# Turning the rows of three norms by DMA on 16-bit planes, in a transformer stack on one Trainium2 core

## The chip, the cores and the metric

One Trainium2 chip, one of its cores. A core has TensorE (PE: matrix products, with results in PSUM), VectorE (DVE), ScalarE (ACT), GpSimd (POOL) and SyncE (SP), which issues DMAs; each engine works through its own queue in order, and they wait for each other through semaphores. The metric is the time of one execution in microseconds (us), as the median of several runs.

## The reference

The input is `x` of 8 sequences x 1024 rows x 256 values, float32. Four layers follow each other, each as a residual over a norm without gain:

```python
x = x + _L0_attn_ref(_layernorm(x), ...)   # linear ("flow") attention + its own FFN of 1024
x = x + _L0_ffn_ref(_layernorm(x), ...)    # relu FFN of 1024
x = x + _L1_attn_ref(_layernorm(x), ...)   # softmax attention over 1024 rows
x = x + _L1_ffn_ref(_layernorm(x), ...)    # gated FFN of 704, operands rounded to blocks of FP4
```

The first layer is a whole decoder layer: attention with cumulative sums along the rows, `h = layernorm(inputs + attn)`, `ffn = gelu(h @ W1 + b1) @ W2 + b2`, and `layernorm(h + ffn)`. All of it is computed in float32 here; only the FP4 rounding uses 16-bit helpers.

## The kernel before

The rows are worked on in chunks of 128 (one row a partition) and in groups of four chunks: 8 sequences x 2 groups = 16 flows. A matmul needs its contraction along the partitions, so a block of rows `[128, 256]` that has just been normed has to be turned into two blocks `[128 features, 128 rows]` before the next layer can multiply it. `turned` does this with two TensorE transpositions against an identity into a PSUM bank, and ScalarE copies the bank into an SBUF tile.

Three such places are touched by the change:

- `linear_chunk`, the first norm after attention: `h` is turned into tile `half` (kind `hT`), the operand of the GELU FFN;
- `norms_1`, the second: `n` is turned into `half` (kind `nT`), the operand of the relu FFN. Both go through `turn_half`;
- `norms_2`, the third: `n` is turned into `n2T`, the operand of the softmax attention, first of all of the values' matmul with `wv3`.

Three other turns stay on TensorE in both kernels: `n0T` ahead of the linear attention, the rows of the FP4 layer, and the probabilities.

`dense` runs both FFNs. For each half group (two chunks, 256 rows) it takes eight steps: a first matmul (`bank<-half,w_in`), an activation into `hidden`, and two steps later a second matmul (`bank<-w_out,hidden`) into an accumulator that is kept over the eight. The weights don't stay in SBUF: each step loads a `w_in` and a `w_out` tile of 128 KB, `W_FF` = 5 tiles of each kind ahead. The linear attention has `V_PADS` = 5 tiles of values, so at most five chunks are between their values and their attention.

Nothing here is scheduled by the hardware or by a compiler. The kernel is written as some hundred Python generators ("parts"), each of which yields what it needs next: an engine, the tiles that must be ready, and how many PSUM banks. `Plan.run` keeps a clock for each engine, made from the costs in `Plan.took`, and picks the part that can go on soonest. `RIPE` says how long an operand should have been ready by that clock, and `at` gives a due time. What is picked is emitted at once, and the order of each engine is pinned to the order of emission. So a cost in `took` doesn't change an instruction; it changes the order. Where the clock sees TensorE pausing for more than 1.6 us, `fill` emits products of the identity with itself that keep the engine running.

Every DMA is issued from SyncE's queue, in order, with eight completion semaphores taken in turn: a DMA also waits for the one that used its semaphore before. In the profile nearly all instructions carry the line of the recording helper (L337), so they are told apart by their tiles.

Of the kernel before, what the change touches and what calls it, by code (L numbers as in the profile page):

```python
# [9 lines left out]
F32 = mybir.dt.float32  # L10
I32 = mybir.dt.int32
BF16 = mybir.dt.bfloat16
AF = mybir.ActivationFunctionType
ALU = mybir.AluOpType
AX = mybir.AxisListType
# [5 lines left out]
FF = 1024  # L21
NF = FF // P
INTER = 704
V_PADS = 5
W_FF = 5
RES = 10
HALVES = 5
LAG = 2
# [24 lines left out]
    "rows": (4, D, F32),  # L53
    "hid": (3, INTER_PAD, F32),
    "q_c": (2, INTER, BF16),
}


# [4 lines left out]
class Plan:  # L63
# [96 lines left out]
    def took(self, queue, op, args, kw):  # L160

        aps = [x for x in list(args) + list(kw.values()) if isinstance(x, bass.AP)]
        outs = [kw["out"] if "out" in kw else aps[0]]
        if kw.get("accum_out") is not None:
            outs.append(kw["accum_out"])
        size = 1
        for ap in aps:
            n = 1
            for d in ap.shape[1:]:
                n *= d  # L170
            size = max(size, n)

        overlap, after = 0.0, 0.035
        if queue == "tensor":
            size = 1
            for d in outs[0].shape[1:]:
                size *= d
            cost = size * (0.853e-3 if op == "transpose" else 1.687e-3)
            tiled = op == "matmul" and (kw["lhsT"].shape[-1] <= 32 or kw["lhsT"].shape[0] <= 32)
            if tiled or op == "matmul" and kw["lhsT"].dtype == BF16:  # L180
                cost *= 0.25
            if tiled != self.tiled:
                cost += 0.2
            self.tiled = tiled
            after = 0.2
        elif queue == "vector":
            each = {"reciprocal": 6.2e-3, "tensor_tensor_scan": 2.15e-3}.get(op, 1.05e-3)
            cost = 0.17 + each * size
            if op == "tensor_scalar" and outs[0].dtype == BF16:
                cost = 0.16 + 0.26e-3 * size  # L190
            elif op == "scalar_tensor_tensor" and any(ap.shape[-1] == 1 for ap in aps):
                cost += 0.06
            overlap = 0.08
        elif queue == "scalar":
            cost = (0.16 if op == "copy" else 0.26) + 0.82e-3 * size
            for x in args:
                if not isinstance(x, bass.AP) and self.SETS.get(x, self.act_set) != self.act_set:
                    self.act_set = self.SETS[x]
                    self.free[queue] = self.free.get(queue, 0.0) + 1.3
            if kw.get("accum_out") is not None:  # L200
                cost += 0.15
            overlap = 0.1
        elif queue == "gpsimd":
            cost = 0.65 + 0.7e-3 * size
            if op in ("tensor_scalar", "iota"):
                cost = 0.22
            elif op == "memset":
                cost = 0.1 + 0.9e-3 * size
        else:
            cost = 0.4  # L210
        start = self.free.get(queue, 0.0)
        if queue not in ("tensor", "sync"):
            start = max([start] + [self.used.get(ap.tensor.name, 0.0) for ap in outs])
        for ap in aps:
            name = ap.tensor.name
            if self.by.get(name) != queue or queue in ("vector", "gpsimd"):
                start = max(start, self.done.get(name, 0.0) + (0.05 if queue == "gpsimd" else 0.0))
            if name not in self.done and name in self.held:
                start = max(start, self.used[name])
        if queue == "tensor":  # L220
            if start - self.ran > 2.0:
                self.slow = start + 2.1
            if start < self.slow:
                cost *= 2
            self.ran = start + cost
        if queue == "sync":
            start = max(start, self.landed.pop(0))
        end = start + cost
        if queue == "sync":
            n = 4e-6 / 250e-3  # L230
            for d in outs[0].shape:
                n *= d
            self.free["rings"] = max(self.free.get("rings", 0.0), end) + n
            after = self.free["rings"] - end + 2.1
            self.landed.append(end + after)
        self.free[queue] = end - overlap
        for ap in outs:
            self.done[ap.tensor.name] = end + after
            self.by[ap.tensor.name] = queue
        for ap in aps:  # L240
            name = ap.tensor.name
            self.used[name] = max(self.used.get(name, 0.0), end + after)
            if queue != "tensor" and name not in self.kept:
                self.held.discard(name)
# [17 lines left out]
    def act(self, *tiles, **kw):  # L262
        return self.need("scalar", tiles, **kw)
# [92 lines left out]
def block_stack_kernel(ctx: ExitStack, tc: tile.TileContext, a: dict, out: bass.AP):  # L356
# [268 lines left out]
    def turned(srcs):  # L625

        bank = tr_bank()
        for i, src in enumerate(srcs):
            nc.tensor.transpose(bank[:, i, :], src, ident)
        return bank[:, : len(srcs), :]  # L630

    def table(func):


        if plan.act_set != plan.SETS.get(func, plan.act_set):
            nc.scalar.activation(small([P, 1], "table", 1), one, func)

    def halves(t):
        return [t[:, 0:P], t[:, P : 2 * P]]
# [259 lines left out]
    def turn_half(p, kind, i, src):  # L899
        dst = half_of(p, kind, i // 2)  # L900
        j = i % 2
        bank = turned(halves(src))
        plan.drop(src)
        yield act(bank)
        nc.scalar.copy(dst[:, :, j * P : (j + 1) * P], bank)
        n = groups[p]["turned"]
        n[kind, i // 2] = n.get((kind, i // 2), 0) + 1

# [218 lines left out]
    def linear_chunk(p, i, n0T, comp, qk):  # L1127
# [171 lines left out]
        for k in range(2):  # L1299
# [8 lines left out]
        plan.drop(u)  # L1308
        yield plan.pool(h)
        nc.gpsimd.tensor_tensor(rc, h, b2, ALU.add)  # L1310
        yield pe(
            h,
            banks=1,
            at=at + 0.74 + 0.06 * i,
            when=lambda: half_fits(p, "hT", i // 2) and count["dense"] >= p - 1,
        )
# [124 lines left out]
    def norms_1(p, i, acc, taken):  # L1441

        s, c = divmod(p * G + i, NCH)
        xc = groups[p]["res"][i]
        xr = yield from fresh("xr", dma())
        nc.sync.dma_start(out=xr, in_=x_dram[s, c * P : (c + 1) * P, :])
        u = yield from fresh("norm", dve(acc, when=lambda: "norms" in late), "u")
        nc.vector.tensor_tensor(u, acc, xc, ALU.add)
        taken()
        stats = ln_stats(u)  # L1450
        yield plan.pool(xr)
        nc.gpsimd.tensor_tensor(xr, xr, ln2b, ALU.add)
        yield from layernorm_affine(xc, u, ln2g, xr, stats)
        plan.drop(u, xr)
        yield dve(xc)
        n = yield from layernorm("norm", xc)
        yield plan.pool(xc, unused=(xc,))
        nc.gpsimd.tensor_tensor(xc, xc, fb2, ALU.add)
        yield pe(n, banks=1, when=lambda: half_fits(p, "nT", i // 2))
        yield from turn_half(p, "nT", i, n)  # L1460

    def norms_2(p, i, acc, taken):

        s, g = divmod(p, NG)
        q, xc = seqs[s], groups[p]["res"][i]
        yield dve(acc)
        nc.vector.tensor_tensor(xc, acc, xc, ALU.add)
        taken()
        yield dve(xc)
        n = yield from layernorm("norm", xc)  # L1470
        kept_rows = hbm.tile([P, D], F32, tag="rows", name="rows", bufs=3 * NCH)
        yield dma(xc)
        nc.sync.dma_start(out=kept_rows, in_=xc)
        q["rows", g * G + i] = kept_rows
        count["res"] -= 1
        yield pe(n, banks=1, when=lambda: s < 2 or count["asked"] >= (s - 1) * NCH)
        if g not in q["n2T"]:
            q["n2T"][g] = two(kept([P, 2 * GT], "n2T", 4))
        n2 = q["n2T"][g]
        here = slice(i * P, (i + 1) * P)  # L1480
        bank = turned(halves(n))
        plan.drop(n)
        yield act(bank)
        nc.scalar.copy(n2[:, :, here], bank)
        yield pe(
            n2,
            banks=1,
            when=lambda: "values" in late and (s < 2 or count["valued"] >= (s - 1) * NCH),
        )
        if g not in q["vt"]:  # L1490
            q["vt"][g] = kept([P, G, D], "vt", 4)
        bank = mm_bank()
        for k in range(2):
            nc.tensor.matmul(
                bank[:, :D], lhsT=n2[:, k, here], rhs=wv3[:, k, :], start=k == 0, stop=k == 1
            )
        yield dve(bank)
        nc.vector.tensor_tensor(q["vt"][g][:, i, :], bank[:, :D], bsv, ALU.add)
        q["normed"] += 1
# [204 lines left out]
```

## Time and profile before

| | |
|---|---|
| time, median of 3 runs | 2633.27 us (2631.56 to 2634.26) |
| span of the profiled execution | 2628.6 us |
| TensorE idle, by its own row | 33.5 us |
| TensorE transpositions of `n` (all four norms that use the name) | 512 |
| TensorE transpositions of `h` | 128 |
| ScalarE copies into `half` and `n2T` | 128 and 64 |
| GpSimd busy | 577.7 us |
| SyncE waiting for TensorE | 1635.6 us in 867 waits |
| DMA traffic | 211.94 MB, mean 81 GB/s |

The profile is of one execution. A row of the groups' table gives engine, operation, output and inputs by their names in the program, shapes, count, busy time and mean duration, and then the engine's idle time before such instructions with what ended it. A float32 matmul stands as two records, a transposition as one. Records of TensorE overlap, so the time that one really holds is read from start to start. Waits are named by the instruction that came last before the waiting one went on.

### The profile page before, as it was taken

The numbers are of one execution on the slowest core, as the hardware profiler recorded it, in microseconds if no ns is written. First come the engines' busy times: TensorE is split into PE (matmuls) and PEld (weight loads), VectorE is DVE, ScalarE is ACT, GpSimd is POOL, SyncE is SP. The second block draws the span as 40 slices with busy tenths as digits, with TensorE's granted clock in tenths as the row PEclk, the third lists the DMA queues.
The fourth block names the chain that finished last, engine by engine and source line by source line (L and its number), as shares of the span: only waits on it lengthen the run. The fifth ranks groups of instructions, "written<-read, shape, count | busy, mean of one in ns | idle before, by whom it ended". The sixth has DMA issues, their size and how long they took to land.

```text
span 2628.6 us, 46432 instructions
## 1 busy us (share of the span) xinstructions
PE 2595.1 (99%) x16891; PEld 2031.8 (77%) x16891; DVE 1924.2 (73%) x4353; ACT 1297.4 (49%) x2665; POOL 577.7 (22%) x1101
## 2 busy tenths in 40 slices
PE   8989999999999999999999999999999999999999
PEld 7777777777777777787777777777787777877777
DVE  7888786868768587685867768686785877755687
ACT  4534445455364554636445364553645545354443
POOL 2333232222212122131221312122121221211000
PEclk9999999999999999999999999999999999999999
DMA  3425333223132232322323223232322312222000
GB/s 94 125 86 155 99 87 103 79 69 107 57 99 73 71 109 62 91 71 76 101 65 98 68 82 85 74 105 63 93 75 69 109 59 87 71 77 81 25 3 22
DMA packets 286819, 211.94 MB, mean 81 GB/s; under 512 B 24704, under 2 KB 275072, under 8 KB 286592
## 3 DMA queue, kind: packets, MB, share of 16 engines
q1 hardware_dynamic: 286592, 208.97, 27.7%
q8 instruction: 135, 2.21, 0.3%
q14 instruction: 92, 0.75, 0.1%
HBM read 188.17 MB, written 20.71 MB: 79 GB/s over the span
## 4 chain that ended last, share of the span: by engine, by line
PE 86%; DVE 8%; DMA 2%; ACT 2%; issue 1%; POOL 0%; SPq 0%; DVEq 0%; POOLq 0%; ACTq 0%
PE bank L337 86%; DVE prod L337 3%; DMA spread<-packed 2%; ACT L337 1%; DVE spread L337 1%; DMA packed<-flow 1%; DVE ln_st L337 0%; DVE u L337 0%; ACT prob L337 0%; DVE hid L337 0%; DVE r L337 0%; DVE res L337 0%; DVE w_raw L337 0%; ACT n0T L337 0%; DVE ln_mv L337 0%
## 5 line engine op out<-in xcount | busy, mean ns | idle before, releaser
L337 PE MATMUL bank<-half,w_in 128*128 128x256 f32 x2048 | 530.5, 382 | 3.6 <-DVE res L337 1.2
L337 PE MATMUL bank<-w_out,hidden 128*128 128x256 f32 x2048 | 532.2, 383 | 0.2 <-ACT hidden L337 0.2
L337 POOL TENSOR_SCALAR ln_ve<-ln_mv 128x1 f32<-128x1 f32 x384 | 97.7, 254 | 1691.8 <-DVE ln_mv L337 1672.4
L337 PEld LDWEIGHTS bank<-w_out,hidden 128*128 128x128 f32 x2048 | 369.5, 190 | 92.7 <-issue 39.7
L337 PEld LDWEIGHTS bank<-half,w_in 128*128 128x128 f32 x2048 | 380.2, 191 | 76.7 <-issue 26.6
L337 ACT ACT_TABLE_LOAD x322 | 413.1, 1283 | 7.9 <-DVE nmax L337 2.0
L337 ACT ACTIVATE hidden<-bank,c_L_ffn_b 128x256 f32<-128x256 f32 x256 | 121.7, 475 | 333.7 <-PE bank L337 333.6
L337 POOL TENSOR_TENSOR ln_rstd<-ln_ve,neghalf 128x1 f32<-128x1 f32 x384 | 238.0, 620 | 32.0
L337 PE MATMUL bank<-n2T,qT 128*128 128x512 f32 x512 | 241.7, 594 | 0.2 <-ACT qT L337 0.2
L337 PE MATMUL bank<-vt,probT 128*128 128x256 f32 x1024 | 231.5, 379 | 0.0
L337 PEld LDWEIGHTS bank<-vt,probT 128*128 128x128 f32 x1024 | 193.4, 190 | 28.3 <-issue 2.4
L337 ACT ACTIVATE hidden<-bank,c_L_attn_b 128x256 f32<-128x256 f32 x256 | 120.2, 470 | 187.0 <-PE bank L337 186.8
L337 PE MATMUL bank<-wdT,hqT 128*128 128x256 f32 x768 | 176.2, 379 | 0.5 <-ACT hqT L337 0.5
L337 PE MATMUL bank<-wgT,xqT 128*128 128x352 f32 x512 | 172.5, 459 | 0.0
L337 PE MATMUL bank<-wuT,xqT 128*128 128x352 f32 x512 | 172.3, 459 | 0.0
L337 DVE TENSOR_TENSOR hid<-hid,bank 128x352 f32<-128x352 f32 x116 | 59.9, 516 | 151.8 <-PE bank L337 124.2
L337 PEld LDWEIGHTS bank<-wdT,hqT 128*128 128x128 f32 x768 | 145.3, 190 | 20.9 <-ACT hqT L337 0.7
L337 DVE TENSOR_TENSOR sc<-bank,triu 128x512 f32<-128x512 f32 x240 | 148.7, 680 | 8.4 <-PE bank L337 7.7
L337 PEld LDWEIGHTS bank<-n2T,qT 128*128 128x128 f32 x512 | 92.8, 190 | 66.9 <-issue 59.8
L337 PEld LDWEIGHTS bank<-wuT,xqT 128*128 128x128 f32 x512 | 97.3, 190 | 54.2
L337 PEld LDWEIGHTS bank<-wgT,xqT 128*128 128x128 f32 x512 | 94.2, 190 | 32.9 <-issue 0.7
L337 DVE TENSOR_REDUCE mx<-bank 128x1 f32<-128x512 f32 x128 | 86.2, 674 | 35.0 <-PE bank L337 35.0
(220 smaller groups left out, 4401.6 us busy)
## 6 DMA issues: line engine op xcount, KB each, us to landing
w_in<-in_L_attn_W_dram SPq DMA_DIRECT2D x256, 128.0 KB
w_out<-in_L_attn_W_dram SPq DMA_DIRECT2D x256, 128.0 KB
w_in<-in_L_ffn_w_dram SPq DMA_DIRECT2D x256, 128.0 KB
w_out<-in_L_ffn_w_dram SPq DMA_DIRECT2D x256, 128.0 KB
spread<-packed SPq DMA_DIRECT2D x90, 256.0 KB
x<-in_L_attn_inputs_dram SPq DMA_DIRECT2D x64, 128.0 KB
xr<-in_L_attn_inputs_dram SPq DMA_DIRECT2D x64, 128.0 KB
rows<-res SPq DMA_DIRECT2D x64, 128.0 KB
```

Source lines behind the costliest of these rows:

```text
L337: ins = method(*args, **kw)
```

## The change

For the three norms, `flip` takes the place of the two transpositions and the copy. The DMA transposition is given 16-bit elements, so a float32 row is first cut into two planes: GpSimd copies the 256 values of a row, seen as 512 16-bit halves, into a tile `cut` with all low halves first and then all high halves. One DMA transposition, issued from SyncE, turns the four 128x128 blocks of `cut` into `spun`. ScalarE copies `spun` into the destination, putting each pair of halves together again; its input is now SBUF and has 512 elements a partition. The bits of each value are unchanged.

`cut` and `spun` have two tiles each, 4 KB a partition in all. `V_PADS` and `W_FF` go from 5 to 4: one tile of values, one of `w_in` and one of `w_out` fewer. `Plan.took` gets a cost for a GpSimd copy and one for the data of a DMA transposition. The needs that the three places yield change from TensorE with a bank to GpSimd, so all of the order that follows is planned anew: of the 2785 rows of TensorE's old order, merged where equal instructions follow each other, the new order has 2591, and it interleaves the work differently throughout.

```diff
--- before.py
+++ after.py
@@ -10,6 +10,7 @@
 F32 = mybir.dt.float32
 I32 = mybir.dt.int32
 BF16 = mybir.dt.bfloat16
+U16 = mybir.dt.uint16
 AF = mybir.ActivationFunctionType
 ALU = mybir.AluOpType
 AX = mybir.AxisListType
@@ -21,8 +22,8 @@
 FF = 1024
 NF = FF // P
 INTER = 704
-V_PADS = 5
-W_FF = 5
+V_PADS = 4
+W_FF = 4
 RES = 10
 HALVES = 5
 LAG = 2
@@ -53,6 +54,8 @@
     "rows": (4, D, F32),
     "hid": (3, INTER_PAD, F32),
     "q_c": (2, INTER, BF16),
+    "cut": (2, 2 * D, U16),
+    "spun": (2, 2 * D, U16),
 }
 
 
@@ -206,6 +209,8 @@
                 cost = 0.22
             elif op == "memset":
                 cost = 0.1 + 0.9e-3 * size
+            elif op == "tensor_copy":
+                cost = 0.15 + 1.0e-3 * size
         else:
             cost = 0.4
         start = self.free.get(queue, 0.0)
@@ -227,7 +232,7 @@
             start = max(start, self.landed.pop(0))
         end = start + cost
         if queue == "sync":
-            n = 4e-6 / 250e-3
+            n = 2e-6 / 150e-3 if op == "dma_start_transpose" else 4e-6 / 250e-3
             for d in outs[0].shape:
                 n *= d
             self.free["rings"] = max(self.free.get("rings", 0.0), end) + n
@@ -628,6 +633,24 @@
         for i, src in enumerate(srcs):
             nc.tensor.transpose(bank[:, i, :], src, ident)
         return bank[:, : len(srcs), :]
+
+    def flip(src, dst):
+
+        cut = yield from fresh("cut", plan.pool(src))
+        nc.gpsimd.tensor_copy(
+            cut.rearrange("p (h f) -> p h f", h=2),
+            src.bitcast(U16).rearrange("p (f h) -> p h f", h=2),
+        )
+        plan.drop(src)
+        spun = yield from fresh("spun", dma(cut))
+        nc.sync.dma_start_transpose(out=spun.rearrange("p (b t) -> p b t", t=P), in_=cut)
+        plan.drop(cut)
+        yield act(spun)
+        nc.scalar.copy(
+            dst.bitcast(U16).rearrange("p k (t h) -> p k t h", h=2),
+            spun.rearrange("p (h k t) -> p k t h", h=2, t=P),
+        )
+        plan.drop(spun)
 
     def table(func):
 
@@ -899,10 +922,7 @@
     def turn_half(p, kind, i, src):
         dst = half_of(p, kind, i // 2)
         j = i % 2
-        bank = turned(halves(src))
-        plan.drop(src)
-        yield act(bank)
-        nc.scalar.copy(dst[:, :, j * P : (j + 1) * P], bank)
+        yield from flip(src, dst[:, :, j * P : (j + 1) * P])
         n = groups[p]["turned"]
         n[kind, i // 2] = n.get((kind, i // 2), 0) + 1
 
@@ -1308,9 +1328,8 @@
         plan.drop(u)
         yield plan.pool(h)
         nc.gpsimd.tensor_tensor(rc, h, b2, ALU.add)
-        yield pe(
+        yield plan.pool(
             h,
-            banks=1,
             at=at + 0.74 + 0.06 * i,
             when=lambda: half_fits(p, "hT", i // 2) and count["dense"] >= p - 1,
         )
@@ -1456,7 +1475,7 @@
         n = yield from layernorm("norm", xc)
         yield plan.pool(xc, unused=(xc,))
         nc.gpsimd.tensor_tensor(xc, xc, fb2, ALU.add)
-        yield pe(n, banks=1, when=lambda: half_fits(p, "nT", i // 2))
+        yield plan.pool(n, when=lambda: half_fits(p, "nT", i // 2))
         yield from turn_half(p, "nT", i, n)
 
     def norms_2(p, i, acc, taken):
@@ -1473,15 +1492,12 @@
         nc.sync.dma_start(out=kept_rows, in_=xc)
         q["rows", g * G + i] = kept_rows
         count["res"] -= 1
-        yield pe(n, banks=1, when=lambda: s < 2 or count["asked"] >= (s - 1) * NCH)
+        yield plan.pool(n, when=lambda: s < 2 or count["asked"] >= (s - 1) * NCH)
         if g not in q["n2T"]:
             q["n2T"][g] = two(kept([P, 2 * GT], "n2T", 4))
         n2 = q["n2T"][g]
         here = slice(i * P, (i + 1) * P)
-        bank = turned(halves(n))
-        plan.drop(n)
-        yield act(bank)
-        nc.scalar.copy(n2[:, :, here], bank)
+        yield from flip(n, n2[:, :, here])
         yield pe(
             n2,
             banks=1,
```

## The prediction

> **What bounds the kernel now.** I read the page first: busy shares, the forty slices, the chain of waits. Then TensorE's own waits, the table of groups with shapes kept apart, the table by stage, and one stretch of the timeline around a norm that the change touches.
>
> ```profile
> span 2628.6 us, 46432 instructions
> PE 2595.1 (99%) x16891; PEld 2031.8 (77%) x16891; DVE 1924.2 (73%) x4353; ACT 1297.4 (49%) x2665; POOL 577.7 (22%) x1101
> PE   8989999999999999999999999999999999999999
> PEclk9999999999999999999999999999999999999999
> PE 86%; DVE 8%; DMA 2%; ACT 2%; issue 1%; POOL 0%; SPq 0%; DVEq 0%; POOLq 0%; ACTq 0%
> ```
>
> TensorE is busy in every slice at full clock, and 86% of the chain that ended last is its own work. A profile can call an engine busy that only overlaps itself, so the next thing is what one transposition holds. The timeline gives it as the distance from one start to the next:
>
> ```profile
> 1046.09 1.03 PE L337 MATMUL bank<-w_out,hidden 128*128 128x256 f32 x4
> 1046.95 1.03 PE L337 MATMUL bank<-half,w_in 128*128 128x256 f32 x4
> 1047.82 0.38 PE L337 MATMUL bank<-ident,n 128*128 128x128 f32 x2
> 1048.04 0.60 PE L337 MATMUL bank<-ident,prob 128*128 128x128 f32 x4
> ...
> 1050.42 1.88 PE L337 MATMUL bank<-n0T,wk 128*128 128x512 f32 x4
> 1052.14 0.38 PE L337 MATMUL bank<-ident,n 128*128 128x128 f32 x2
> 1052.35 1.03 PE L337 MATMUL bank<-w_out,hidden 128*128 128x256 f32 x4
> 1053.22 0.38 PE L337 MATMUL bank<-ident,n 128*128 128x128 f32 x2
> 1053.44 1.88 PE L337 MATMUL bank<-n0T,wq 128*128 128x512 f32 x4
> ```
>
> Start to start, two transpositions take 1048.04 - 1047.82 = 0.22 us, 0.11 each, although the table of groups calls one 275 ns long (the records overlap); four matmuls of 256 columns take 0.86, 0.215 each. Over the whole trace the median start to start of a transposition is 0.109 us. The stretch also shows the third norm: an accumulation ends near 1047.1 (the first line), its two rows are turned at 1052.14 and 1053.22, and the first matmul that reads them stands at 1057.74. So the turned rows are used 5.6 us after the first transposition, and TensorE never stopped in between.
>
> ```profile
> 0.00:130.00 130.00, 118.21 (x965) 95.86 (x965) 100.60 (x252) 63.28 (x160) 37.03 (x77) 1.00 0.39 107
> 330.00:2300.00 1970.00, 1962.15 (x12973) 1536.92 (x12973) 1447.90 (x3232) 1001.39 (x2012) 446.56 (x844) 1.00 0.28 82
> ```
>
> By stage (columns: length, then busy time of PE, PEld, DVE, ACT, POOL, clock, DMA share, GB/s): idle TensorE is at the start, 12 us in the first 130, and under 8 us in the 1970 of the middle. The kernel is TensorE work end to end, in an order fixed before it runs.
>
> **What the Trainium skill says.** "VectorE: DVE Perf Modes", section The three transpose paths: a 128x128 16-bit block takes 390 ns on TensorE into PSUM, 1309 ns by the DMA crossbar into SBUF. The trace has TensorE's at 275 ns for float32, 109 in steady flow; it shows no crossbar. "DMA: Bandwidth & Descriptors", section DMA Transpose (X-bar): two-byte types alone, which explains the two planes; no run here shows it. "Advanced Engine Details and Errata", section X-Bar Transpose (TRN2): such DMAs are as fast as regular ones, 350 to 400 GB/s. "SBUF — State Buffer", section Who interferes with whom: GpSimd and VectorE lock a shared port against each other; the trace agrees faintly, the same GpSimd addition of 128x256 taking 742 to 922 ns by group.
>
> **The change part by part.**
>
> *Removed:* 2 transpositions for each of 64 chunks and 3 norms, 384 of TensorE: 384 x 0.109 = 41.9 us. Their mean start to start is 0.128, so up to 384 x 0.019 = 7.3 us of waiting stood behind them; I count 3 of it as gone. Also 192 ScalarE copies of 128x256 from PSUM (371 to 380 ns) and 192 short holds of a PSUM bank, which nothing waits for.
>
> *Added, GpSimd:* 192 copies of 512 16-bit elements. The nearest row is the copy of 256 float32, 397 ns; between 0.4 (by bytes) and 0.8 us (by elements), I take 0.7: 134 us on an engine with 578 of 2629 busy. Nothing of it lies on TensorE's path, but it stands in GpSimd's queue before the reciprocal roots of other norms (VectorE waited 44 us for these), and when both cut tiles are still being read, GpSimd waits for a landing with those roots behind it. Cost 0 to 10 us; in the waits below.
>
> *Added, ScalarE:* 192 copies of 512 elements in place of 256: 0.59 us (the 128x512 copies, 589 to 598 ns) for 0.37, 42 us on an engine 49% busy. Hidden, but each waits for a landing at the head of ScalarE's queue, and the hidden activation behind it feeds TensorE three matmul groups later.
>
> *Added, SyncE:* 192 DMAs of 131 KB, each behind the weight loads. SyncE's plain issues take 0.33 to 0.6 us and the queue waits 1636 us for TensorE to free weight tiles, so there is room. From issue to landing nothing in the trace is a transposition. Nearest, in the chain of waits: 2.7 to 3.0 us for the 64 KB writes of packed, 3.3 to 5.2 for the 256 KB reads of spread. Below: 131 KB at 350 GB/s, 0.4 us, added to the some 2.1 us that are left of a small one, 2.5 (an estimate from the errata page). Above: four blocks in a row at 1309 ns, 5.2 us, behind an issue and a receipt of 2 us together, over 7 (an estimate from the VectorE page). I take 3.5.
>
> *Fewer tiles:* weights are loaded 4 tiles ahead instead of 5. 512 steps lie between 60 and 2444 us, 4.7 us a step, so a load has over 18 us of lead; where the steps are densest a step is eight matmul records, 1.73 us, and four are 6.9 us, against landings of 2 to 6 us. Cost 0, cover gone if landings pass 7 us. Value tiles: 4 chunks ahead; a chunk comes each 41 us. 0.
>
> *The new order.* I laid the start-to-start times over the order in which each kernel queues its TensorE work. Work between the last matmul of an accumulation and the first matmul that reads the turned block (least / middle): for the third norm 10.6 / 14.9 us (before 5.2 / 10.8), for the second 15.4 / 24.0 (12.2 / 23.8), for the first 6.4 / 37.3 (3.7 / 44.7). From the same accumulation's end to the end of VectorE's normalised row the trace of before has in the middle and at nine tenths: 5.0 / 8.4, 11.9 / 13.4, 3.3 / 7.8. What remains must hold the new path: 0.7 copy + 3.5 landing + 0.6 copy + 0.3 for handing over = 5.1 us. Third norm: 14.9 - 5.0 = 9.9, enough; 11.6 (its lowest tenth) - 8.4 = 3.2, short by 1.9. Second: 24.0 - 11.9 = 12.1, enough. First: enough but at the start. So about a fifth of the 32 pairs of the third norm wait some 1.5 us, with a few more: I take 8 us.
>
> *The start.* The new order holds 137 filler transpositions of the identity, the old one 94, all the new ones within the first 1000 matmuls: the first rows come later there. A filler is two records, 0.218 us: 43 x 0.218 = 9.4 us, and four new pauses whose first 0.7 us the code leaves unfilled, 3 us.
>
> **Sum:** 2628.6 - 41.9 - 3 + 9.4 + 3 + 8 = 2604 us of span. The median of the runs, 2633.27, lies 4.7 above the profiled span; so 2609.
>
> **Rivals.**
>
> *The landing sets the end (slower).* Place: the third norm, where the order leaves 9.9 us in the middle. If a transposition lands after 8 us, the path is 9.6: rows whose VectorE part took 8.4 miss by 3.1 and the middle ones just fit, some 2 us in each of 32 pairs, 64 us, and 10 from the second norm: 2609 - 8 + 74 = 2675. At 10 us it is near 2780. It decides from about 6.5 us, where the waits (1 us a pair, over 30) eat the 30 that were won. For it: the 1309 ns a block, three in-order queues with a waiting instruction at their head, weight loads behind a transposition on SyncE. Against: the crossbar's bandwidth, a quiet DMA (28% busy in the middle). Chance 0.34.
>
> *All of it is kept.* Landings as fast as a weight load, the start no worse in fact than before: 2633.3 - 45 = 2588. For it: pauses foreseen need not come. Chance 0.12.
>
> *Given back.* TensorE waits for exactly what it no longer does, since another chain (VectorE at 73%, the spread rows in the linear attention) was due at the same time: 2633. The chain of waits has 8% VectorE and 2% DMA, mostly between stretches of TensorE, so little of it is ready to take over. Chance 0.06.
>
> *The forecast,* 2596 to 2628: 0.48.
>
> **How the numbers follow.** Within 0.2% (5.3 us) no measurement of this kernel tells a change. Faster: 0.48 + 0.12 = 0.60; same 0.06; slower 0.34. The range from 2588 to 2690 leaves out some 0.04 below and 0.14 above, the landings over about 8.5 us. Cases of both signs hold much of the chance, so the likeliest one's own range: 2596 to 2628.
>
> **What would show it.** Right: TensorE's instructions down by 298 records (384 less 86), idle TensorE in the middle stage at 8 to 20 us, transpositions landing in 3 to 4.5 us, no wait of TensorE on half or n2T above a few us in total. Wrong: TensorE or ScalarE waiting for spun many times over, GpSimd's idle time ended by DMA, SyncE's transposition issues above 1.5 us, or VectorE waiting longer for the reciprocal roots.

## The result, and the profile after

The changed kernel takes 2614.8 us in the median of 4 runs (2614.64 to 2618.8), the kernel before on the same chip 2632.91. The ratio is 0.9936 with a 95% interval of 0.9922 to 0.995: 17 us faster, where 24 were forecast from the profiled spans and 41.9 us of transpositions were taken off TensorE.

The head of the page after:

```profile
span 2617.1 us, 46326 instructions
...
PE 2571.5 (98%) x16593; PEld 2010.4 (77%) x16593; DVE 1947.3 (74%) x4352; ACT 1344.0 (51%) x2658; POOL 703.0 (27%) x1293
...
PE   8998999999999999999999999999999999999999
...
PE 80%; DVE 13%; ACT 3%; DMA 1%; issue 1%; POOL 1%; SPq 0%; DVEq 0%; POOLq 0%; ACTq 0%
```

TensorE has 298 records fewer, as counted from the order (384 less 2 x 43), and is busy 23.6 us less. But the span is only 11.5 us shorter: idle TensorE went from 33.5 to 45.6 us. In the chain that ended last, VectorE's share went from 8% to 13% and ScalarE's from 2% to 3%. The work that is gone from TensorE didn't all become time; a part became waiting. (The profiled execution is the slowest of the four: 2618.8 us, the three others about 2614.7 with spans of 2613.)

Its trace also has more time at half clock: 13.7 us ahead of the end in place of 6.8, which costs a TensorE that is always busy up to half of the difference, 3.4 us. Two of the stretches, of 3.41 us each, begin 0.6 us after TensorE took up work again from a pause of 2.08 and of 1.88 us. So a pause can cost more than its length, but not each does: none follows the longest pause after the first 100 us, 2.84 us at 232.

Where it waits, by the same stages as before (length, then busy time of PE, PEld, DVE, ACT, POOL, clock, DMA share, GB/s):

```profile
0.00:130.00 130.00, 118.26 (x951) 96.36 (x952) 92.74 (x234) 60.67 (x151) 39.94 (x81) 0.97 0.37 99
130.00:330.00 200.00, 186.95 (x1493) 150.19 (x1492) 161.99 (x368) 100.91 (x216) 73.55 (x131) 0.99 0.50 132
330.00:2300.00 1970.00, 1954.78 (x12746) 1525.97 (x12745) 1478.61 (x3264) 1033.49 (x2004) 553.19 (x1007) 1.00 0.34 93
```

The second row of the kernel before, which was not shown above, is:

```profile
130.00:330.00 200.00, 190.16 (x1486) 150.71 (x1485) 159.86 (x366) 86.21 (x202) 62.15 (x113) 0.98 0.40 115
```

The first 130 us are as idle as before (11.7 against 11.8 us), though more of what is busy at the start is filler. The next 200 have 13.1 us of idle TensorE, before 9.8, and the middle 15.2, before 7.9.

The pieces of the new path, first from the view of the tile `spun` (duration in ns, least/middle/most):

```profile
L342 SPq DMA_TRANSPOSE spun<-cut x192: 1188/1197/2336, 56.4 to 2437.6; - x192
L342 ACT COPY half<-spun x128: 656/675/694, 59.6 to 2387.5; 128x512 uint16<-128x512 uint16 x128
L342 ACT COPY n2T<-spun x64: 661/670/692, 157.6 to 2443.2; 128x512 uint16<-128x512 uint16 x64
```

and from that of the tile `cut`:

```profile
L342 POOL COPY cut<-n x128: 602/613/1607, 107.3 to 2436.5; 128x512 uint16<-128x512 uint16 x128
L342 POOL COPY cut<-h x64: 599/609/1014, 55.4 to 2289.5; 128x512 uint16<-128x512 uint16 x64
```

And one of them in the timeline:

```profile
708.99 0.61 POOL L342 COPY cut<-h 128x512 uint16<-128x512 uint16 x1
709.62 1.20 SPq L342 DMA_TRANSPOSE spun<-cut  x1
712.04 0.68 ACT L342 COPY half<-spun 128x512 uint16<-128x512 uint16 x1 [3.03 <-DMA spun<-cut]
```

The copy ends at 709.60, the transposition is issued at 709.62 and has landed before 712.04, 2.4 us later, and the rows are in place at 712.72: 3.7 us from the start of GpSimd's copy to the end of ScalarE's. That is the shortest of the 192; the middle one takes 4.8 us, nine tenths take up to 7.2. The bracket says that ScalarE had stood still for 3.03 us, and that the landing ended it. Over all 192, by the completion records in the trace, issue to landing takes 2.47 us in the middle and 4.0 at nine tenths. Nearly half of the middle one is SyncE's own issue.

What waited, first in the view of TensorE's waits (total us, times, longest):

```profile
PE bank L342 <- DVE kv L342: 4.8, 3, 1.9
PE bank L342 <- DVE v L342: 4.5, 4, 1.5
...
PE bank L342 <- ACT n2T L342: 3.7, 3, 2.1
...
PE bank L342 <- ACT half L342: 1.4, 1, 1.4
```

then in the view of all engines' waits:

```profile
ACT half L342 <- DMA spun<-cut: 149.6, 82, 5.1
...
ACT n2T L342 <- DMA spun<-cut: 20.3, 12, 3.6
```

ScalarE stands 170 us waiting for landings, while TensorE is charged with only 5 us of waiting for the turned rows themselves. Two readings fit: the standing ScalarE delays the other work in its queue, or TensorE's rows come so closely on time that small delays spread over many neighbours. (Of the 128 places where TensorE turns to newly turned rows, 64 half groups of the FFNs and 64 chunks of values, 7 start within 0.1 us of the end of ScalarE's copy.) The experiments had to decide.

### The profile page after: what moved, and what is told of

It is laid out like the page before. It is cut to its first block, busy times and chain, and to the rows that moved or that the text cites. A ratio compares the mean times of both kernels' runs of the same rounds, so it can differ in the third digit from the quotient of the medians.

```text
span 2617.1 us, 46326 instructions
## 1 busy us (share of the span) xinstructions
PE 2571.5 (98%) x16593; PEld 2010.4 (77%) x16593; DVE 1947.3 (74%) x4352; ACT 1344.0 (51%) x2658; POOL 703.0 (27%) x1293
## 3 DMA queue, kind: packets, MB, share of 16 engines
q1 hardware_dynamic: 391040, 234.16, 33.1%
## 4 chain that ended last, share of the span: by engine, by line
PE 80%; DVE 13%; ACT 3%; DMA 1%; issue 1%; POOL 1%; SPq 0%; DVEq 0%; POOLq 0%; ACTq 0%
PE bank L342 80%; DVE hid L342 2%; DVE prod L342 2%; DVE n L342 1%; ACT L342 1%; DVE ln_st L342 1%; DVE u L342 1%; DVE res L342 1%; DVE ln_mv L342 0%; DVE x_amax L342 0%; DMA spread<-packed 0%; DVE div L342 0%; DVE spread L342 0%; DVE mx L342 0%; DMA spun<-cut 0%
## 5 line engine op out<-in xcount | busy, mean ns | idle before, releaser
L342 ACT COPY half<-spun 128x512 uint16<-128x512 uint16 x128 | 86.3, 674 | 150.1 <-DMA spun<-cut 149.6
```

Source lines behind the costliest of these rows:

```text
L342: ins = method(*args, **kw)
```

## The experiments

Every time is compared with runs of the kernel before that were measured beside it, with medians of 2631.0 to 2631.8 us. A difference between two ratios of 0.0010 is 2.6 us; intervals are some 0.0013 to either side, a little less where there were more runs.

**What the path costs, without a new order.** In these kernels the planner is told of everything that the changed kernel does, so the order of TensorE and VectorE is its order to the instruction, but GpSimd's copy and the DMA transposition aren't issued, and ScalarE copies the rows unturned.

```diff
-        nc.gpsimd.tensor_copy(cut..., src.bitcast(U16)...)
+        plan.took("gpsimd", "tensor_copy", (cut..., src.bitcast(U16)...), {})
-        nc.sync.dma_start_transpose(out=spun..., in_=cut)
+        plan.took("sync", "dma_start_transpose", (), {"out": spun..., "in_": cut})
-        nc.scalar.copy(dst.bitcast(U16)..., spun...)
+        plan.emit("scalar", "copy", (dst, src), planned=(dst.bitcast(U16)..., spun...))
```

> The order of the changed kernel on TensorE and VectorE, to the instruction, but without the path: no GpSimd copy and no DMA transposition is issued, and ScalarE copies the normed rows as they are into half and n2T (256 float32 a partition from SBUF), at the place where it copied spun. What is left out: the rows aren't turned, so all that follows works on unturned blocks. Theory A (the path's length costs: turned rows reach TensorE late, and ScalarE, GpSimd and SyncE stand behind waits for them): TensorE's waits after the first 260 us go from 51 us back towards 33, and the time falls by 10 to 20 us to about 2600. Theory B (the path costs nothing, the loss lies in the new order, with its 43 fillers and fewer tiles): 2610 to 2616, within 5 us of the changed kernel.

Measured: 2599.3 us, ratio 0.9878 (0.9865 to 0.9892), 15 us faster than the changed kernel by the ratios.

```profile
span 2599.0 us, 45756 instructions
...
PE 2564.2 (99%) x16593; PEld 2005.9 (77%) x16593; DVE 1932.5 (74%) x4352; ACT 1287.5 (50%) x2658; POOL 572.8 (22%) x1101
```

Idle TensorE went from 45.6 to 34.7 us, about what the kernel before has. Theory A holds: the path costs 15 us. Without it, 32 us are gained, and that is what the order promises, 41.9 less 9.4 for the fillers. So these two terms hold almost all of the account: 41.9 = 9.4 fillers + 15 path + 17 gained.

The path is more than its length, though. VectorE's 4352 instructions are the same in both kernels, yet take 1932.5 us here and 1947.3 with the path; of the 14.8 us, 13.8 stand in the 322 instructions that overlap a copy into `cut`. So the copies of GpSimd lengthen VectorE's work. How much of that reaches TensorE, no run separates from the lateness of the rows.

The same leaving-out, for one part of the norms at a time (`flip` for the others):

```diff
-        yield from flip(n, n2[:, :, here])                            # e9
+        yield from flip_ghost(n, n2[:, :, here])
-        yield from flip(src, dst[:, :, j * P : (j + 1) * P])          # e10
+        yield from flip_ghost(src, dst[:, :, j * P : (j + 1) * P])
```

> The changed kernel's order on TensorE, VectorE and ScalarE to the instruction, with the path (GpSimd copy, DMA transposition) left out for the third norm alone; its 64 row blocks reach n2T unturned, the other two norms go by DMA. No new planning, so no luck of an order in it. Theory A3 (the waits belong to the third norm): 10 us or more faster than the changed kernel, about 2603. Theory A12 (they belong to the first and second, as the two runs with norms left on TensorE suggest): 0 to 5 us faster, 2610 to 2615.

> The same, with the path left out for the first and second norm (half gets unturned rows), and kept for the third. Theory A3: 0 to 5 us faster than the changed kernel. Theory A12: 10 to 14 us faster, about 2602. If the two runs together give the 15 us of the run without any path, the waits add up; if each alone gives most of them, they share one cause (SyncE's or ScalarE's queue).

Measured: 2611.4 us, ratio 0.9924 (0.9911 to 0.9936), and 2602.8 us, ratio 0.9893 (0.9878 to 0.9909). That is 3 and 11 us faster than the changed kernel; the 3 alone is inside the intervals, the 11 is not. Together they make 14 of the 15 of the first run. By the times, most of the price goes away with the path of the first and second norm, the operands of the FFNs. The traces below show that it isn't all paid at their own rows.

**SyncE's issue time.**

```diff
-        nc.sync.dma_start_transpose(out=spun..., in_=cut)
+        nc.sync.as_if_transposed(out=spun..., in_=cut...)   # a plain dma_start, planned as the other
```

> The changed kernel in the same order, with a plain DMA of the same 131 KB from cut to spun in place of the transposition. What is left out: the planes aren't turned. The issue should take some 0.4 us of SyncE in place of 1.19, the landing some 2.2 in place of 2.5. Theory C (SyncE's issue time holds back the weight loads and other transfers behind it): 5 to 12 us faster than the changed kernel, waits of TensorE for w_in and w_out gone. Rival (SyncE has room): within 3 us of 2615.

Measured: 2611.2 us, ratio 0.9923 (0.991 to 0.9935).

```profile
L345 SPq DMA_DIRECT2D spun<-cut x192: 464/471/946, 56.6 to 2430.3; - x192
```

The issue took 0.47 us, and the landing 2.03 in the middle by the completion records (2.47 in the changed kernel). 3 us faster by the ratios, within the intervals. That three quarters of a microsecond per issue hold back the weight loads isn't shown; at most it is a small part of the 15.

**ScalarE standing at the head of its queue.** The order of the other engines stays; each copy of `spun` is emitted later in ScalarE's queue.

```diff
-        nc.scalar.copy(dst.bitcast(U16)..., spun...)
+        plan.copy_later(dst.bitcast(U16)..., spun...)   # after up to two more activations,
+                                                        # before the first reader of dst
```

> The changed kernel with nothing left out and the same order on TensorE, VectorE, GpSimd and SyncE; on ScalarE each copy of spun stands one to five instructions further back (three in the middle), behind up to two activations, never behind the first reader of its half or n2T. Theory H (a copy that waits for its landing at the head of ScalarE's queue holds up the work behind it; ScalarE waited 170 us for spun): 4 to 10 us faster, ScalarE's waits for spun under 60 us. Theory L (what costs is that the turned rows themselves reach TensorE late): the same or 1 to 5 us slower.

Measured: 2647.2 us, ratio 1.0067 (1.0054 to 1.0079): 34 us slower than the changed kernel, and slower than the kernel before. From its view of all waits:

```profile
PE bank L365 <- ACT half L260: 17.9, 20, 2.0
...
PE bank L365 <- ACT n2T L260: 12.9, 14, 2.2
...
ACT n2T L260 <- DMA spun<-cut: 9.2, 5, 3.1
...
ACT half L260 <- DMA spun<-cut: 4.3, 5, 2.8
```

ScalarE now waits 13.5 us for landings in place of 170, just as theory H wanted, and TensorE waits 31 us for the rows in place of 5. Theory H falls, at least as something that a later place could mend. ScalarE stood at the head of its queue for what TensorE needed next. A few instructions more on the way, and TensorE stops by name: the path from the start of GpSimd's copy to the end of ScalarE's is 8.1 us in the middle here, 4.8 in the changed kernel, and 36 of the 128 places now start within 0.1 us of the copy's end, in place of 7. The direction is that of theory L, the size isn't: it had allowed 1 to 5 us, and 34 were paid for 3.2 us of path.

That a longer path is dear doesn't yet say what the 15 us of the changed kernel were paid for. But TensorE's 16593 records stand in the same order in all these kernels, so two traces can be laid side by side and the added time read before each matmul (us; one execution each, the slowest of its four for the changed kernel):

| | in all | in the first 260 us | before `bank<-wv,n2T` | before `bank<-half,w_in` | before `bank<-w_out,hidden` |
|---|---|---|---|---|---|
| changed, over the one without the path | 18.1 | 9.4 | 6.8 | 5.2 | -0.6 |
| changed, over the one without the third norm's path | 7.4 | 4.1 | 5.4 | 3.0 | 0.3 |
| changed, over the one without the first two norms' | 13.3 | 6.2 | 5.1 | 4.3 | -0.3 |
| copies later, over changed | 29.4 | 1.6 | 13.3 | 19.3 | 0.0 |

Two thirds of the price, 12 of 18 us, stand before the matmuls that read turned rows, and nothing before those that read `hidden`, where theory H would have it. That is what theory L says; the other third is scattered, and its cause stays open. About half of the price falls within the first 260 us. And the values' matmul with `wv3`, which reads the third norm's rows, loses most of its 6.8 us of delay in either of the two partial runs, also where the third norm itself still goes by DMA. This fits rows of the three norms that wait for each other in the same queues, which no run tested by itself.

**The fewer tiles.**

```diff
-V_PADS = 5
-W_FF = 5
+V_PADS = 4
+W_FF = 4
```

> The kernel before with 4 value tiles and 4 tiles of each weight, nothing else. Theory D (the fewer tiles ate part of the gain): 2640 to 2646, waits of TensorE for weights. Rival (the lead is enough, as forecast): 2631 to 2637, the 12 more fillers of its order (2.6 us) included.

Measured, as an edit of the kernel before: 2637.2 us, ratio 1.0022 (1.0014 to 1.003), 6 us slower, of which 2.6 are its 12 fillers. It lies at the edge between the two expectations: a small cost that I had put at nothing. Whether it is paid in the changed kernel too was not tried. The first run, which also has the fewer tiles, gains what the order promises; a cost of the tiles can hide there only if something else was gained beside, such as the waits that had stood behind the old transpositions.

**The luck of an order.**

```diff
-            each = {"reciprocal": 6.2e-3, "tensor_tensor_scan": 2.15e-3}.get(op, 1.05e-3)
+            each = {"reciprocal": 6.2e-3, "tensor_tensor_scan": 2.15e-3}.get(op, 1.051e-3)
```

> The changed kernel with VectorE's cost in the planner 0.1% higher (1.051 for 1.05 ns an element): the same work and the same 137 fillers in another order. This is the measure of how much a mere new order moves the time. If orders scatter little: 2611 to 2619. If a good part of the result is the luck of an order: outside 2605 to 2625.

Measured: 2620.2 us, ratio 0.9952 (0.9939 to 0.9966): 4 us slower than the changed kernel, the intervals overlapping; it fell between the two expectations. The same work in another order can move the time by some 4 us, as far as one other order tells. Differences of this size between two newly planned kernels mean nothing.

**One part of the change at a time.**

```diff
-            yield from flip(...)          # for the norms left out of the part
+            bank = turned(halves(n))
+            yield act(bank)
+            nc.scalar.copy(dst, bank)
```

> Only the third norm (n2T) goes by DMA; the first two stay on TensorE; tiles as in the changed kernel. TensorE's work by its order: 128 transpositions less (14.0 us) and 12 fillers more (2.6), 11.3 us less than before. Theory A3 (the path's 15 us of waits belong mostly to the third norm, where the order leaves least room, as forecast): some 10 us of new waits, 2628 to 2633 on a kernel of before at 2631. Rival A-even (each norm brings a third of the waits): 2623 to 2627.

> The first and second norm by DMA, the third on TensorE. TensorE's work by its order: 256 transpositions less (27.9 us) and 44 fillers more (9.6), 18.3 us less than before. Theory A3: few new waits, 2612 to 2617. Rival A-even: 10 us of new waits, 2620 to 2625.

Measured: the third norm alone 2627.5 us, ratio 0.9987 (0.9981 to 0.9994); the first two 2636.1 us, ratio 1.0015 (1.0009 to 1.0022). The first fell between the two theories. Neither foresaw the second: TensorE has 18.3 us less to do than in the kernel before, and the kernel is 4 us slower. Its idle TensorE is 46.2 us. It points the same way as the runs that keep the order (the first two norms are the dear ones), but by more: 11 us is the path's price there, and 11 more are missing. The fewer tiles and this kernel's own order are candidates; how it divides stays open, and it shows that a new plan can give back more than the repetition above let expect. The two parts together gain nothing by these runs, the whole gains 17: parts of a change to a planned kernel can't be summed.

**Less of it where it hurts, and a better plan.** The first three of sixteen groups stay on TensorE (e7); then, beside that, the planner gets what the profile shows (e8).

```diff
+FLIPS = 3                                    # norms of groups 0 to 2: turned on TensorE
-            cost = 0.4
+            cost = 1.2 if op == "dma_start_transpose" else 0.4     # this and all below: e8 alone
-            after = self.free["rings"] - end + 2.1
+            after = self.free["rings"] - end + (1.93 if op == "dma_start_transpose" else 2.1)
+            if outs[0].dtype == U16:
+                cost = 0.68
```

> The changed kernel, but the first three of the sixteen groups have their rows turned on TensorE as before, and the DMA path begins with the fourth. 72 of the 384 transpositions come back (7.8 us), and the fillers go from 137 to 106 (6.8 us): nearly the same work. Theory S (the new path also makes real waits at the start, beyond the fillers): 3 to 6 us faster than the changed kernel. Rival (the start's waits in fact are no longer than before, 38.5 against 36 us in the first 260): within 3 us of it.

> As the one before, and the planner is told what the profile shows: a transposition holds SyncE's queue 1.2 us, lands 4.0 us after its issue (the slow tenth; the middle is 2.5), and ScalarE's copy of spun takes 0.68 us. The same instructions in an order with more room behind each transposition. If the waits behind the path come from an order that expected the rows sooner: 5 to 12 us faster than the changed kernel, waits after 260 us near 40. If they come from collisions that no cost foresees: within 4 us of the one before.

Measured: 2607.4 us, ratio 0.9909 (0.9893 to 0.9924), and 2603.6 us, ratio 0.9893 (0.9879 to 0.9906). The first is 7 us faster than the changed kernel with 1 us more of TensorE's work; the intervals just touch, but the place fits: the traces put 9 us of the price into the first 260. The second is 11 us faster than the changed kernel, clear of the intervals. Against the first its 4 us are no more than an order's luck, so both of its expectations fit and it doesn't decide between them. Its profile:

```profile
span 2600.6 us, 46220 instructions
...
PE 2566.7 (99%) x16603; PEld 2000.6 (77%) x16603; DVE 1948.7 (75%) x4352; ACT 1329.7 (51%) x2642; POOL 693.7 (27%) x1257
```

Idle TensorE is 33.9 us, as before the change, with the path in place for thirteen of sixteen groups; it was 39.3 with the start alone. So the waits aren't a property of the path alone: 7 of the 15 us went with the start, where 72 of the 384 transpositions had been. That the planner's truer costs helped is not shown.

With that order, the rows of the FP4 layer were moved as well, a fourth turn of 128 transpositions:

```diff
-        yield pe(n, banks=1, at=at + 0.5, when=lambda: "fp4" in weights)
-        bank = turned(halves(n))
-        plan.drop(n)
-        xqT = two((yield from fresh("soft", act(bank), "xqT")))
-        nc.scalar.copy(xqT, bank)
+        need = plan.pool(n, at=at + 0.5, when=lambda: "fp4" in weights)
+        xqT = two((yield from fresh("soft", need, "xqT")))
+        yield from flip(n, xqT)
```

> The kernel of the run before last but three (start on TensorE, landing planned at 4.0 us) with one more turn moved: the rows of the FP4 layer (xqT, 64 chunks, 128 transpositions more off TensorE, 14.0 us; 106 fillers as there). If the path's price per row block is that of the third norm (3 us for 64 blocks): about 2594 to 2598 on a kernel of before at 2631. If it is that of the first two (11 us for 128) or the turn is tighter still, since each soft chunk is one long chain: 2600 to 2606, no gain over 2603.

Measured: 2593.0 us, ratio 0.9855 (0.9839 to 0.9871): 38 us faster than the kernel before, 21 faster than the changed one.

```profile
span 2590.7 us, 46216 instructions
...
PE 2550.6 (98%) x16475; PEld 1989.7 (77%) x16475; DVE 1950.0 (75%) x4352; ACT 1350.6 (52%) x2649; POOL 719.8 (28%) x1321
```

Of 14.0 us taken off, about 10 became time, clear of the intervals. The price of the path for 64 more blocks, 4 us, is like the third norm's 3, though both are of the size of an order's luck.

## Why the prediction was right, and where not

Right in direction, and the median lies 6 us off, but that closeness is in part luck, since two errors of the sum cancel in it. The sum gave a span of 2604; the profiled one is 2617.1, the other three are 2613: 9 to 13 us too little. The 4.7 us that I added from span to median were 1.7 here: if the same 1.7 hold before, the profiled execution there was itself some 3 us quicker than the median. One of my signs of being wrong came true: ScalarE waited for `spun` 94 times, 170 us in all.

- *384 x 0.109 = 41.9 us off TensorE, 43 fillers for 9.4.* Held: 298 records fewer, and the run without the path gains 32 us, the difference of the two.
- *The path takes 5.1 us from normed row to turned row.* Near in the middle, too short where it counted. The pieces were off in both directions: GpSimd 0.61 in the middle and 0.73 on average (0.7 taken), ScalarE 0.675 (0.59), issue to landing 2.47 in the middle (3.5). They add up to 3.8 us, but each stands in a queue: from the end of VectorE's row to the end of ScalarE's copy the trace has 5.8 us in the middle and 8.4 at nine tenths. The bound below, 2.5, was nearly the middle; the 4.0 at nine tenths fell within the two bounds. The statement of the Trainium skill ("Advanced Engine Details and Errata", X-Bar Transpose (TRN2)) that such a DMA is as fast as a regular one nearly fits for the landing: a plain one in the same place landed after 2.03 us, and SyncE's issue, longer by 0.73, is more than the whole difference of 0.44. It doesn't fit for what the transfer occupies (last section).
- *8 us of waits, from the third norm; 3 us of old waits gone.* The failed step. The waits cost 15, and leaving out the third norm's path gives back 3 of these, leaving out the path of the first two 11, whose room I had called enough but at the start. I compared least and middle of the room with middle and nine tenths of VectorE's part, one at a time. For the second norm, the middle room was 24.0 and VectorE's part at nine tenths 13.4 by the trace of before; after the change it is 17.8 at nine tenths, since the new order fills VectorE's queue differently; it isn't the path, for without it the figure is 17.4, and VectorE's waits for the reciprocal roots didn't grow (42 us, before 44). 24.0 - 17.8 - 5.1 leaves 1 us, and with the path's own slow tenth, 8.4, the row is late. The middle of the distribution hides this, and that both rows of a pair must be there.
- *Fewer tiles: 0.* In the kernel before they cost 6 us with fillers. For the changed kernel it stays open.
- *SyncE has room.* Held: a plain, short issue in the same place gains 3 us at most. The issue itself I had put at 0.33 to 0.6; it is 1.19.
- *The start: 3 us beyond the fillers.* Too little: by the traces laid side by side, 9 us of the path's price fall within the first 260 us, and the run that keeps the start on TensorE is 7 us faster.
- *The slow rival, a landing from 6.5 us on.* Didn't come: landings stay under 5.5. But its mechanism was the right one: the run with the copies some three places later shows what happens when the path gets longer, 34 us for 3.2 in the middle.

## What to carry to other kernels

Work moved off the bounding engine is worth its start-to-start time there, not its listed duration (0.109 us, not 0.275), less what the longer path makes that engine wait. In a kernel with a fixed order, leave the old path where nothing covers the new one (here the first groups), and when you ask whether a row comes in time, set the slow tenth of the new path and of what stands before it against the room, not the middle. Giving the planner the measured durations is the obvious next step, but here its 4 us can't be told from an order's luck. To see what a path costs, take it out and keep the order; to take one part of a change out and let the order be made anew measures the order as well. And where two kernels share an order, lay their traces side by side: the added time stands before the instructions that pay it.

## What the hardware showed that I hadn't expected

A DMA transposition of 131 KB holds SyncE's queue for 1.19 us, a plain DMA of the same tiles 0.47. And it travels in small pieces: the page before and the page after (in this order) differ by 104448 packets under 512 B, 544 for each of the 192.

```profile
DMA packets 286819, 211.94 MB, mean 81 GB/s; under 512 B 24704, under 2 KB 275072, under 8 KB 286592
...
DMA packets 391268, 237.11 MB, mean 91 GB/s; under 512 B 129152, under 2 KB 379520, under 8 KB 391040
...
q1 hardware_dynamic: 391040, 234.16, 33.1%
```

What the transfers occupy is read against the kernels of the same order without the path and with the plain DMA:

```profile
q1 hardware_dynamic: 286592, 208.97, 28.1%
...
q1 hardware_dynamic: 314240, 234.15, 30.6%
```

28.1% of 2599.0 us, 30.6% of 2610.2 and 33.1% of 2617.1 are 730, 799 and 866 us of all sixteen DMA engines. So the plain DMA took some 0.36 us of them for each 131 KB, the transposition 0.71 (an estimate from the shares). That is 185 GB/s for the transposition, where the Trainium skill, in the section named above, has 350 to 400; the plain one comes to 368. In landing time the two are close, in occupied engines the transposition costs twice as much; the measurement decides. With the queue at a third in all, the engines were far from full.
